# An LSTM step on one core: ScalarE writes tanh(c) into the PSUM bank of c instead of SBUF

## The chip, the cores and the metric

The kernel runs on one core of a Trainium2 chip. The metric is the device time of one execution in microseconds (us), lower is better. The engines of the core are named as in the profile: PE is the matrix engine TensorE (PEld its weight loads), DVE is VectorE, ACT is ScalarE, POOL is GpSimd, SP is the queue that issues most DMAs.

## The reference

An LSTM over a sequence of 1024 steps for a batch of two, with 256 hidden units, and behind it a mixture of experts; both are added to their inputs.

```
def step(carry, xw_t):
    prev_h, prev_c = carry
    a = xw_t + prev_h @ Wh              # 2 x 1024: gates i, f, o, g
    i, f, o = sigmoid of the first three quarters of a
    g = tanh(a[:, 3 * Hdim:])
    next_c = f * prev_c + i * g
    next_h = o * jnp.tanh(next_c)
    return ((next_h, next_c), next_h)
x = x + LSTM(x, h0=cond)                # the scan of step over 1024 steps
x = x + MoE(x, cond)                    # 2 shared and 8 routed experts, top 2
```

All arithmetic is float32. What matters here is the last line of the step: the next h is o times the tanh of the new c, and the next step can't begin its matmuls before it has h.

## The kernel before, in words

The 256 hidden units lie in two halves of 128 partitions (index m, 0 or 1). Of every half the four gates of one step stand in one PSUM tile, ps0 and ps1, 32 columns to a step's row block; 16 steps share one pair of tiles (u counts them, 0 to 15).

One step t goes through the engines like this:

- PE (L504): 20 matmuls in the order BLOCKS (L42) multiply h by Wh and add to the projected input. Each is two passes in the trace, hence 40 records of a step. The first two blocks need only the first half of h (k = 0); the third, (1, 0, 0, 128), is the first that needs the second half of h. The third ends what ps0 needs, the fifth what ps1 needs.
- DVE (L529): two transposes, ps0 and then ps1, each into the other half of the same PSUM bank.
- ACT (L532, L533): for each half the sigmoid of i, f, o and the tanh of g, read from PSUM and written into the SBUF tile `results`.
- DVE, for each half: `forget` (L536) multiplies f by the old c, which it reads from PSUM; a copy (L540, tile `seen`) waits for the tanh of g; a scan (L541) writes the new c into a PSUM tile of its half, `c0` or `c1`.
- ACT (L549, `squash_cell`): tanh of the new c, read from PSUM, written into the SBUF tile `results`. This is the line that the change touches.
- DVE (L552, `output`): o times that tanh, written into the SBUF tile h, from which PE loads the weights of the next step.

DVE has the order first forget, copy, scan; second forget, copy, scan; first output, second output. ACT has the two tanh of c behind the four activations of the gates. Both engines work strictly in the order of the code, and the waits between engines are semaphores that are counted up when an instruction is done.

c has two slots in its tile, for even and odd steps, so that the old and the new c stand side by side. The two tiles `c0` and `c1` lie in two PSUM banks of their own; the gates take four banks and the experts' work two, which makes all eight.

The experts run in the gaps. A small planner, `Fill`, keeps three queues; at each step it emits some expert matmuls for PE behind the step's own (and otherwise matmuls of zeros, L518, up to ROOM = 2 a step), some activations behind the tanh of c on ACT, and some vector work behind the outputs on DVE. A fixed budget for each step limits them. Once in 16 steps ACT also zeroes a part of the next `results` tile (L479), and POOL adds the input to h (L455).

Of the kernel before, what the change touches and what calls it, by code (L numbers as in the profile page):

```python
# [9 lines left out]
F32 = mybir.dt.float32  # L10
BF16 = mybir.dt.bfloat16
AF = mybir.ActivationFunctionType
# [4 lines left out]
P = 128  # L17
N = 2
T = 1024
D = 256  # L20
K = D // P
Q = 4
ROWS = P // Q
TB = ROWS // N
# [61 lines left out]
def lstm_moe_kernel(  # L86
# [16 lines left out]
    nc = tc.nc  # L103
# [58 lines left out]
    cells_ps = ctx.enter_context(tc.tile_pool(name="cells_ps", bufs=1, space=PSUM))  # L162
    stepp = ctx.enter_context(tc.tile_pool(name="step", bufs=3))
    stepsp = ctx.enter_context(tc.tile_pool(name="steps", bufs=2))
# [255 lines left out]
    for i in range(2):  # L420
        flat = const.tile([P, TB * DIAG], F32, name=f"h{i}")
# [4 lines left out]
    def h_at(t):  # L426
        return hs[t // TB % 2][:, t % TB]

    def h_cols(t):
        u = t % TB  # L430
        return h_at(t)[:, :, N * u : N * (u + 1)]
# [3 lines left out]
    def project(ps, grp, k):  # L435
        for m in range(K):
            for q in range(Q):
                cols = slice(q * D + m * P, q * D + (m + 1) * P)
                nc.tensor.matmul(  # L439
                    ps[m][q * ROWS : (q + 1) * ROWS],  # L440
                    one_sb if k < 0 else xT_sb[:, k, grp * TB : (grp + 1) * TB, :],
                    b_sb[:, cols] if k < 0 else wx_sb[:, k, cols],
                    start=(k < 0),
                    stop=False,
                    skip_group_check=True,
                )

    def gates_tile():

        tiles = [gates_ps.tile([P, 4, P], F32, name=f"ps{m}") for m in range(K)]  # L450
        return [a[:, 0] for a in tiles], [a[:, 1] for a in tiles], tiles[0][:, 2:]

    def residual(grp, u0, u1):
        t0 = grp * TB - 1
        nc.gpsimd.tensor_add(  # L455
            x2T[:, :, t0 + u0 : t0 + u1, :],
            xT_sb[:, :, t0 + u0 : t0 + u1, :],
            diags[grp % 2][:, u0:u1].rearrange("p u (k r) -> p k u r", r=ROWS)[:, :, :, :N],
        )
# [12 lines left out]
    nc.vector.memset(zero, 0.0)  # L472

    def results():
        flat = stepsp.tile([P, TB, K, 9 * N], F32, name="results")
        sgm = flat[:, :, :, : 6 * N].rearrange("p u m (a n z) -> p u m a n z", n=N, z=2)
        gf = flat[:, :, :, 6 * N : 8 * N].rearrange("p u m (n z) -> p u m n z", z=2)
        for m in range(K):
            nc.scalar.activation(sgm[:, :, m, 0, :, 0], zero[:, :, m], AF.Copy)  # L479
        return sgm, gf, flat[:, :, :, 8 * N :]  # L480

    nxt_results = results()

    cells = [cells_ps.tile([P, 2, N, 2], F32, name=f"c{m}") for m in range(K)]
    c_prev = [cells[m][:, 1] for m in range(K)]
    for m in range(K):
        nc.vector.memset(cells[m], 0.0)
# [5 lines left out]
    for t in range(T):  # L493
        fill.step = t
        grp, u = divmod(t, TB)
        if u == 0:
            ps, turned = nxt, nxt_turned
            nxt, nxt_turned, busy = gates_tile()
            sgm, gf, tnh = nxt_results


        for k, m, c0, c1 in BLOCKS:
            for q in range(Q):
                nc.tensor.matmul(  # L504
                    ps[m][q * ROWS : (q + 1) * ROWS][:, c0:c1],
                    h_at(t)[:, k, :],
                    wh_sb[:, k, q * D + m * P + c0 : q * D + m * P + c1],
                    start=False,
                    stop=(u == TB - 1 and k == K - 1),
                    skip_group_check=True,  # L510
                )
        ahead = t + TB < T and u in (1, 6, 11)
        if ahead:
            project(nxt, grp + 1, u // 5 - 1)
        left = max(1, due - t)
        done = fill.run_pe(-(-len(fill.pe) // left))
        for _ in range(ROOM - done - ahead):
            nc.tensor.matmul(  # L518
                busy.rearrange("p a j -> p (a j)"), busy_x[:, :P], busy_x,
                start=(u == 0), stop=False, skip_group_check=True,  # L520
            )
        rows = slice(N * u, N * (u + 1))

        gT = [turned[m].rearrange("p (a r) -> p a r", r=ROWS) for m in range(K)]
        c_new = [cells[m][:, t % 2] for m in range(K)]
        seen = [stepp.tile([P, N], F32, name=f"seen{m}") for m in range(K)]

        def transpose(m):
            nc.vector.transpose(turned[m], ps[m])  # L529

        def squash(m):
            nc.scalar.activation(sgm[:, u, m, :, :, 1], gT[m][:, 0:3, rows], AF.Sigmoid)  # L532
            nc.scalar.activation(gf[:, u, m, :, 0], gT[m][:, 3, rows], AF.Tanh)  # L533

        def forget(m):
            nc.vector.tensor_mul(gf[:, u, m, :, 1], sgm[:, u, m, 1, :, 1], c_prev[m][:, :, 1])  # L536

        def cell(m):

            nc.vector.tensor_copy(seen[m], gf[:, u, m, :, 0])  # L540
            nc.vector.tensor_tensor_scan(  # L541
                c_new[m].rearrange("p n z -> p (n z)"),
                sgm[:, u, m, 0].rearrange("p n z -> p (n z)"),
                gf[:, u, m].rearrange("p n z -> p (n z)"),
                0.0, ALU.mult, ALU.add,
            )

        def squash_cell(m):
            nc.scalar.activation(tnh[:, u, m], c_new[m][:, :, 1], AF.Tanh)  # L549

        def output(m):
            nc.vector.tensor_mul(h_cols(t + 1)[:, m], sgm[:, u, m, 2, :, 1], tnh[:, u, m])  # L552

        for fn in (transpose, squash):
            for m in range(K):
                fn(m)
        for m in range(K):
            forget(m)
            cell(m)
            squash_cell(m)  # L560
        for m in range(K):
            output(m)
        if u == TB // 2 and t + TB < T:
            nxt_results = results()
        else:
            fill.run(fill.act, 1.0)
        c_prev = c_new
        if u == TB - 1:
            residual(grp, int(grp == 0 or t - TB in ends), TB)
        if t in ends:  # L570
            residual(grp + 1, 0, 1)
            if t == T - 1:
                drain(fill)
            t0, S = ends[t]
            experts(t0, S)
            due = t + S
        if u == TB // 2 and t > TB:

            met = stepp.tile([P, 1], F32, name="met")
            nc.vector.tensor_copy(met, x2T[:, 0, t - u - 2, :1])  # L580
        fill.run(fill.dve, 0.5)
# [3 lines left out]
def drain(fill):  # L585

    while fill.pe or fill.act or fill.dve:
        fill.step += 1
        fill.run_pe(4)
        fill.run(fill.act, 100.0)  # L590
        fill.run(fill.dve, 100.0)
# [65 lines left out]
```

## Time and profile before

| | us |
|---|---|
| median of three runs | 2358.14 (2358.02 to 2358.67) |
| the execution that was profiled | 2357.18 |
| its span, first to last instruction | 2355.4 |
| PE busy | 2260.8 |
| DVE busy | 1717.5 |
| ACT busy | 917.2 |

The span has four parts: some 19 us until the first step's h, the 1024 steps up to 2299 us, and then some 56 us in which the experts of the last 64 positions are worked off. The granted clock of TensorE was 0.998 over the whole.

How to read it: PE counts as busy for nearly the whole span, but a large part of that are the matmuls of zeros and the overlapped ends of pipelined matmuls. The step is a loop through three engines, so the shares of busy time say little here; what counts is how long it takes from one h to the next. A timeline lists instructions by their start and duration, in us; in an answer on one line of code, the three durations are the least, the median and the largest in ns.

### The profile page before, as it was taken

The page shows a single profiled execution, that of the slowest core. Times are in us where ns is not written, and L with a number is a line of the kernel's source. Part 1 is how long each engine was busy: PE and PEld are TensorE (multiplying, and loading weights), DVE is VectorE, ACT ScalarE, POOL GpSimd, SP SyncE. Part 2 cuts the span into 40 slices and gives each one's busy share as a digit, 9 for nine tenths or more (in the row PEclk, how much of TensorE's full clock was granted, in tenths as well). Part 3 has the DMA queues.
Part 4 walks back from the last instruction along what each step waited for, and adds up shares of the span by engine and source line. Part 5 has one row for each costly group of instructions (what it writes and reads, how often), then busy time and mean ns, then how long its engine had stood idle before and what let it go on. Part 6 is the DMA issues. An engine that isn't in the chain of part 4 may idle for free.

```text
span 2355.4 us, 114090 instructions
## 1 busy us (share of the span) xinstructions
PE 2260.8 (96%) x48164; PEld 1604.7 (68%) x48164; DVE 1717.5 (73%) x10962; ACT 917.2 (39%) x6427; POOL 25.8 (1%) x82
## 2 busy tenths in 40 slices
PE   7999999999999999999999999999999999999998
PEld 5666666666666666666666666666666666667777
DVE  5666677777777777777777777777777777777774
ACT  3333334433444334443334433443334433344341
POOL 0000000000000000000000000000000000000000
PEclk9999999999999999999999999999999999999999
DMA  5000000000000000000000000000000000000000
GB/s 199 3 3 3 3 3 3 3 5 6 3 3 3 5 5 3 3 3 5 6 3 3 3 5 5 3 3 3 5 5 3 3 3 5 5 3 3 8 3 5
DMA packets 9412, 20.95 MB, mean 9 GB/s; under 512 B 1473, under 2 KB 6593, under 8 KB 8642
## 3 DMA queue, kind: packets, MB, share of 16 engines
q1 hardware_dynamic: 8610, 12.61, 1.5%
q8 instruction: 376, 6.16, 1.1%
q14 instruction: 138, 1.13, 0.2%
q10 hardware_dynamic: 288, 1.05, 0.1%
HBM read 11.56 MB, written 2.10 MB: 6 GB/s over the span
## 4 chain that ended last, share of the span: by engine, by line
DVE 58%; PE 39%; issue 3%; DMA 0%; SPq 0%; ACT 0%; ACTq 0%
PE ps L504 35%; DVE ps L529 28%; DVE c L541 11%; DVE results L536 8%; DVE seen L540 7%; DVE h L552 3%; PE ps_f L292 1%; PE ps_f L372 1%; PE ps_f L354 1%; DMA xT_sb<-in_xT_dram 0%; DMA wr_sb<-in_wrT_dram 0%; PE ps_f L348 0%; PE ps L518 0%; DVE acc L382 0%; PE ps L439 0%
## 5 line engine op out<-in xcount | busy, mean ns | idle before, releaser
L504 PE MATMUL ps<-wh_sb,h 128*32 128x128 f32 (+1 forms) x40960 | 1116.1, 254 | 72.4 <-DVE h L552 2.2
L504 PEld LDWEIGHTS ps<-wh_sb,h 128*32 128x32 f32 x40960 | 840.8, 109 | 477.2 <-DVE h L552 476.0
L529 DVE STREAM_TRANSPOSE ps<-ps 128x128 f32<-128x128 f32 x2048 | 676.7, 331 | 414.3 <-PE ps L504 413.1
L532 ACT ACTIVATE results<-ps 128x6 f32<-128x6 f32 x2048 | 362.5, 177 | 1178.7 <-DVE ps L529 1085.8
L518 PE MATMUL ps<-busy_x 128*128 128x256 f32 x2080 | 613.5, 392 | 0.0
L552 DVE TENSOR_TENSOR h<-results 128x2 f32<-128x2 f32 x2048 | 327.3, 160 | 175.0 <-ACT results L549 174.9
L518 PEld LDWEIGHTS ps<-busy_x 128*128 128x128 f32 x2080 | 375.4, 190 | 87.0 <-issue 46.6
L549 ACT ACTIVATE results<-c 128x2 f32<-128x2 f32 x2048 | 352.6, 172 | 205.2 <-DVE c L541 165.4
L541 DVE TENSOR_TENSOR_SCAN c<-results 128x4 f32<-128x4 f32 x2048 | 359.8, 176 | 0.0
L533 ACT ACTIVATE results<-ps 128x2 f32<-128x2 f32 x2048 | 343.5, 168 | 0.0
L540 DVE COPY seen<-results 128x2 f32<-128x2 f32 x2048 | 332.4, 162 | 0.0
L536 DVE TENSOR_TENSOR results<-results,c 128x2 f32<-128x2 f32 x2048 | 322.5, 157 | 0.0
L292 PE MATMUL ps_f<-x2T,w_sb 128*128 128x256 f32 (+1 forms) x576 | 177.0, 406 | 4.2 <-DVE h_s L315 3.4
L292 PE MATMUL ps_f<-x2T,r_sb 128*128 128x256 f32 (+1 forms) x576 | 172.5, 398 | 1.2 <-DVE h_r L335 1.0
L372 PE MATMUL ps_f<-r_sb,h_r 128*128 128x256 f32 x512 | 165.9, 421 | 0.0
L292 PEld LDWEIGHTS ps_f<-x2T,w_sb 128*128 128x128 f32 x576 | 84.8, 195 | 51.0 <-issue 46.2
L292 PEld LDWEIGHTS ps_f<-x2T,r_sb 128*128 128x128 f32 x576 | 82.5, 189 | 46.9 <-issue 45.1
L372 PEld LDWEIGHTS ps_f<-r_sb,h_r 128*128 128x128 f32 x512 | 80.4, 188 | 43.4 <-issue 39.6
L439 PE MATMUL ps<-wx_sb,xT_sb 128*32 128x128 f32 x2048 | 80.1, 275 | 3.0 <-DMA xT_sb<-in_xT_dram 3.0
L354 PE MATMUL ps_f<-w_sb,h_s 128*128 128x256 f32 x256 | 82.7, 420 | 0.0
L382 DVE SCALAR_TENSOR_TENSOR acc<-ps_f,gate,acc 128x256 f32<-128x256 f32 x128 | 61.3, 479 | 7.2 <-PE ps_f L372 6.9
L439 PEld LDWEIGHTS ps<-wx_sb,xT_sb 128*32 128x32 f32 x2048 | 59.1, 111 | 3.4 <-issue 3.4
(60 smaller groups left out, 435.1 us busy)
## 6 DMA issues: line engine op xcount, KB each, us to landing
xT_sb<-in_xT_dram SPq DMA_DIRECT2D x8, 256.0 KB, 6.5
r_sb<-in_r_w1T_dram SPq DMA_DIRECT2D x1, 2048.0 KB, 16.7
r_sb<-in_r_w2T_dram SPq DMA_DIRECT2D x1, 2048.0 KB, 18.8
out_dram<-acc SPq DMA_DIRECT2D x16, 128.0 KB, 2.1
wh_sb<-in_wh_dram ACTq DMA_DIRECT2D x2, 512.0 KB, 4.0
wx_sb<-in_wx_dram SPq DMA_DIRECT2D x2, 512.0 KB, 5.3
w_sb<-in_s_w1T_dram SPq DMA_DIRECT2D x1, 1024.0 KB, 7.2
w_sb<-in_s_w3T_dram SPq DMA_DIRECT2D x1, 1024.0 KB
```

What stands on the lines that cost most here:

```text
L292: nc.tensor.matmul(ps[:, half, :W], w[:, k, c * P : (c + 1) * P], mov[k], start=(k == 0), stop=(k == K - 1), skip_group_check=True,)
L372: nc.tensor.matmul(ps[:, half, :], toks(st["h_r"][:, c, :], i), r2_sb[:, c, :], start=(h == 0), stop=(h == HR // P - 1), skip_group_check= ...
L504: nc.tensor.matmul(ps[m][q * ROWS : (q + 1) * ROWS][:, c0:c1], h_at(t)[:, k, :], wh_sb[:, k, q * D + m * P + c0 : q * D + m * P + c1], sta ...
L518: nc.tensor.matmul(busy.rearrange("p a j -> p (a j)"), busy_x[:, :P], busy_x, start=(u == 0), stop=False, skip_group_check=True,)
L529: nc.vector.transpose(turned[m], ps[m])
L532: nc.scalar.activation(sgm[:, u, m, :, :, 1], gT[m][:, 0:3, rows], AF.Sigmoid)
L533: nc.scalar.activation(gf[:, u, m, :, 0], gT[m][:, 3, rows], AF.Tanh)
L536: nc.vector.tensor_mul(gf[:, u, m, :, 1], sgm[:, u, m, 1, :, 1], c_prev[m][:, :, 1])
L540: nc.vector.tensor_copy(seen[m], gf[:, u, m, :, 0])
L541: nc.vector.tensor_tensor_scan(c_new[m].rearrange("p n z -> p (n z)"), sgm[:, u, m, 0].rearrange("p n z -> p (n z)"), gf[:, u, m].rearrang ...
L549: nc.scalar.activation(tnh[:, u, m], c_new[m][:, :, 1], AF.Tanh)
L552: nc.vector.tensor_mul(h_cols(t + 1)[:, m], sgm[:, u, m, 2, :, 1], tnh[:, u, m])
```

## The change

The tanh of c no longer goes to the SBUF tile `results` but to a third slot of the PSUM tile of c of the same half, and the output multiply reads it there. The row of `results` shrinks from 18 to 16 floats for each step and half. A second, separate edit concerns the matmuls of zeros: of the two that stand in the first step of a group, only the first now has the flag that starts a fresh sum in the bank, and none has it behind a projection that has already set it.

```diff
     def results():
-        flat = stepsp.tile([P, TB, K, 9 * N], F32, name="results")
+        flat = stepsp.tile([P, TB, K, 8 * N], F32, name="results")
-        gf = flat[:, :, :, 6 * N : 8 * N].rearrange("p u m (n z) -> p u m n z", z=2)
+        gf = flat[:, :, :, 6 * N :].rearrange("p u m (n z) -> p u m n z", z=2)
...
-        return sgm, gf, flat[:, :, :, 8 * N :]
+        return sgm, gf
...
-    cells = [cells_ps.tile([P, 2, N, 2], F32, name=f"c{m}") for m in range(K)]
+    cells = [cells_ps.tile([P, 3, N, 2], F32, name=f"c{m}") for m in range(K)]
...
-            sgm, gf, tnh = nxt_results
+            fresh = True
+            sgm, gf = nxt_results
...
             project(nxt, grp + 1, u // 5 - 1)
+            fresh = False
...
-                start=(u == 0), stop=False, skip_group_check=True,
-            )
+                start=fresh, stop=False, skip_group_check=True,
+            )
+            fresh = False
...
         def squash_cell(m):
-            nc.scalar.activation(tnh[:, u, m], c_new[m][:, :, 1], AF.Tanh)
+            nc.scalar.activation(cells[m][:, 2, :, 0], c_new[m][:, :, 1], AF.Tanh)
 
         def output(m):
-            nc.vector.tensor_mul(h_cols(t + 1)[:, m], sgm[:, u, m, 2, :, 1], tnh[:, u, m])
+            nc.vector.tensor_mul(h_cols(t + 1)[:, m], sgm[:, u, m, 2, :, 1], cells[m][:, 2, :, 0])
```

## The prediction, made before the run

> **What bounds the kernel now.** I read the chain of waits first, then the groups by line, then the timeline of one ordinary step, then the start and duration of every record of the lines of the step (all ns below are medians or means over those 1,024 steps).
>
> ```profile
> DVE 58%; PE 39%; issue 3%; DMA 0%; SPq 0%; ACT 0%; ACTq 0%
> ...
> L552 DVE TENSOR_TENSOR h<-results 128x2 f32<-128x2 f32 x2048 | 327.3, 160 | 175.0 <-ACT results L549 174.9
> ...
> L549 ACT ACTIVATE results<-c 128x2 f32<-128x2 f32 x2048 | 352.6, 172 | 205.2 <-DVE c L541 165.4
> ```
>
> The chain is the loop from h to h, 2,220 ns in the median step, and the page gives ACT no share of it. That is the first thing to test, since the change makes nothing but ACT's tanh of c (L549) and its reader (L552) different. One step, DVE and then ACT:
>
> ```profile
> 1001.23 0.66 DVE L529 STREAM_TRANSPOSE ps<-ps 128x128 f32<-128x128 f32 x2 [0.55 <-PE ps L504]
> ...
> 1002.14 0.16 DVE L536 TENSOR_TENSOR results<-results,c 128x2 f32<-128x2 f32 x1
> 1002.21 0.16 DVE L540 COPY seen<-results 128x2 f32<-128x2 f32 x1
> 1002.33 0.17 DVE L541 TENSOR_TENSOR_SCAN c<-results 128x4 f32<-128x4 f32 x1
> 1002.41 0.16 DVE L552 TENSOR_TENSOR h<-results 128x2 f32<-128x2 f32 x1
> 1002.74 0.16 DVE L552 TENSOR_TENSOR h<-results 128x2 f32<-128x2 f32 x1 [0.17 <-ACT results L549]
> ```
>
> ```profile
> 1002.21 0.17 ACT L549 ACTIVATE results<-c 128x2 f32<-128x2 f32 x1
> 1002.53 0.17 ACT L549 ACTIVATE results<-c 128x2 f32<-128x2 f32 x1 [0.16 <-DVE c L541]
> ```
>
> The second output (1002.74) starts 32 ns behind the end of the second tanh: it waits for ACT, plainly. The first output (1002.41) starts 83 ns behind the start of the second scan in every ordinary step (82 to 85), so the page puts it down to DVE. But in the same records it also starts only 32 to 39 ns behind the end of the first tanh. Which of the two holds it? Its end tells: by how early the first tanh was, the steps sort into
>
> - gap of 33 ns to the tanh's end: duration 160, end 243 behind the scan's start (113 steps)
> - gap of 35: duration 159, end 242 (336 steps)
> - gap of 37: duration 156, end 239.5 (50 steps)
> - gap of 38: duration 156, end 239 (36 steps)
>
> The end stays 193 to 194 ns behind the tanh's end, whatever the start. So **the first output is held by ACT too**, by its end though not by its start, and a shorter tanh would bring h earlier. How far, steps show in which the tanh had long been done: 22 times the second scan took 254 to 258 ns in place of 175, and the output behind it then had a duration of 143 to 145 and ended 59 ns behind the scan's end; in steps 0 and 1 it ended 58 and 62 behind. Ordinary steps have 66.8. So DVE itself would let go of h **7.8 ns** earlier, and no more.
>
> From h, PE's loads follow at once: 53 ns behind the end of the first output in nearly all steps. The third block needs the second half of h, and here is a second, small stall: where the second output ends up to 277 ns behind that first load, the step's last matmul starts at +815; above that it slips ns for ns (280: +818). The mean is 279.4, the mean slip **2.4 ns** a step.
>
> **The change part by part.** By the two kernels' lists of instructions no instruction is added, removed or moved on any engine, and each keeps the semaphore it waits for. There are 2,048 tanh with another destination and 2,048 multiplies with another source.
>
> *The multiply.* `forget` (L536) already has the form that L552 gets: one operand in SBUF, the other in PSUM, 128x2, output to SBUF, held by ACT.
>
> ```profile
> L536 DVE TENSOR_TENSOR results<-results,c x2048: 143/157/160, 18.5 to 2298.9; 128x2 f32<-128x2 f32 x187
> ...
> L552 DVE TENSOR_TENSOR h<-results x2048: 143/160/164, 19.1 to 2299.5; 128x2 f32<-128x2 f32 x187
> ```
>
> From the end of the activation to its own end `forget` takes 190 ns, L552 193.5. I take -3.5 ns for each multiply. [...] The rows of this trace differ: 157 with PSUM against 160 without.
>
> *The tanh.* No row has ACT writing PSUM, so its price is bounded from both sides. What ACT saves when its source is PSUM: the sigmoid L236 reads SBUF and takes 208 ns for 16 elements; L309 to L330 (378 ns at 256 elements, 592 at 512) give 0.84 ns an element, so 195 remain; L549 from PSUM has 172 - 2 = 170. That is 25 ns; were the destination worth as much, the tanh would take 147. On the other side DVE: its scan, which writes PSUM, ends 92 ns behind the next start (175 - 83), its multiply, which writes SBUF, 83 (160 - 77, to the work behind the second output), so a write to PSUM costs DVE 9 or 10 ns more. I take a gain of 15 ns, nearer to the row of the same engine; the bounds are +25 and -10. [...]
>
> *The sum for one step.* The first tanh ends 48 ns behind the second scan's start, the output 193.5 later: 242. After: 48 - 15 + 190 = 223, but DVE allows no less than 242 - 7.8 = 234. The gain is 7.8; any tanh shorter by 4 ns gives it all. The second output ends 15 + 3.5 earlier, the first load 7.8 earlier, so the second is 10.7 earlier against it, 268.7 in place of 279.4: under 277, and the 2.4 ns of PE's stall go too (from 7 ns of gain on). Together 10.2 ns. What is late next is the second scan, through the second transpose: it stands on PE's last matmul and on the first transpose, which come 10.2 earlier with everything else, and on no part of ACT that changes.
>
> Steps that have it: all but the 22 with the long scan, which have only the 2.4, and about 20 of the last 64, which take 2.5 to 2.9 us because expert matmuls fill PE. That leaves some 980 steps: 980 x 10.2 = **10.0 us**. The drain of 56 us behind the last step is not touched.
>
> *At nothing:* the memset of c grows from 8 to 12 columns (65 ns now, twice, while the first loads are under way); uncovered it is some 8 ns once. The flag of the zero matmuls changes no duration that a row distinguishes. The rows of `results` are 64 bytes apart in place of 72; medians by place in the group differ by 1 or 2 ns in L532 and L536, which is 2 us either way and stands in the range.
>
> On the profiled execution 2357.18 - 10.0 = 2347.2; it lies 1.0 under the median of the runs, so the median should go from 2358.14 to **2348**.
>
> **The rivals.**
>
> 1. *The destination is worth nothing to ACT, or the page is right that ACT is off the chain.* With 0 from the tanh only the 3.5 of the multiply stay, 3.4 us: 2354.7. If the second scan alone held the first output, the 2.4 of PE alone would go: 2355.8. Against the second reading stands the row of gaps and ends; nothing excludes the first.
> 2. *ACT's write to PSUM is answered later* (slower than before). The price is DVE's 10 ns. Both outputs then come 10 - 3.5 = 6.5 later, and nothing hides it, since DVE's own floor is passed: 6.4 us, 2364.5; without the 3.5, 2368. It decides as soon as the tanh is over 4 ns longer than now. For it: ACT would read and write the same bank, which no row shows.
> 3. *VectorE is late on a PSUM operand that another engine has just written.* The transposes start 68 ns behind the modelled end of PE's last matmul, 35 more than the 33 that DVE has behind ACT. Then 48 - 15 + 193.5 + 35 = 262, 20 over now: 2378. Against it: ACT starts 33 ns behind DVE's writes to PSUM. [...]
> 4. *DVE's floor is lower.* The shortest multiplies take 143; at a start of +83 that ends at 226, not 234: 16 + 2.4 ns, 18 us, 2340. It needs a gain of 12 or more from the tanh.
>
> **How the numbers follow.** Forecast 0.55, with its own range 2344 to 2351 (the floor of 58 to 62 ns, the 2 us of the rows of `results`); rival 1 0.17, rival 2 0.15, rival 3 0.06, rival 4 0.07. Faster by over 0.2% (4.7 us, about what a measurement of this kernel can tell from no change) are the forecast and rival 4, 0.62; within it rival 1, 0.17; slower rivals 2 and 3, 0.21. The range is 2340 to 2365: it leaves out rival 3 and the upper part of rival 2.
>
> **What would show it.** In the profile after: the tanh at some 157 ns (147 to 182 are the bounds); the output's durations under 160, the first one's near 150, and its start still 83 behind the second scan; the end of the first output 234 behind that start; the second output under 277 ns behind the first load; the median step near 2,210 ns. A tanh of 172 makes it rival 1, of 180 rival 2; a gap from tanh to second output well over 32 ns rival 3. I am wrong if the first output's end is not ACT's to move, or if the tanh is no shorter.

## The result and the profile after

The changed kernel takes **2345.62 us** in the median of six runs (2344.69 to 2346.22), the kernel before 2358.13 in six runs beside it: a ratio of 0.9946, 95% interval 0.9933 to 0.9959. That is 12.5 us less; 10.0 were forecast. The profiled execution took 2345.25 us, span 2343.5, against 2357.18 and 2355.4: 11.9 less.

The page after, chain of waits and groups by line (the tanh of c is now L552, the output L555, the transposes L532, PE's step matmuls L505):

```profile
DVE 58%; PE 38%; issue 3%; DMA 1%; ACT 0%; SPq 0%; ACTq 0%
...
L555 DVE TENSOR_TENSOR h<-results,c 128x2 f32<-128x2 f32 x2048 | 313.8, 153 | 168.4 <-ACT c L552 168.3
...
L552 ACT ACTIVATE c<-c 128x2 f32<-128x2 f32 x2048 | 321.5, 157 | 220.0 <-DVE c L544 180.1
```

The chain gives ACT 0% before and after, although nothing but ACT's instruction and its reader got faster: the mean tanh went from 172 ns to 157, the mean output from 160 to 153. One step in the timeline, DVE and then ACT:

```profile
1001.40 0.17 DVE L544 TENSOR_TENSOR_SCAN c<-results 128x4 f32<-128x4 f32 x1
1001.48 0.15 DVE L555 TENSOR_TENSOR h<-results,c 128x2 f32<-128x2 f32 x1
1001.80 0.16 DVE L555 TENSOR_TENSOR h<-results,c 128x2 f32<-128x2 f32 x1 [0.17 <-ACT c L552]
```

```profile
1001.28 0.16 ACT L552 ACTIVATE c<-c 128x2 f32<-128x2 f32 x1
1001.61 0.16 ACT L552 ACTIVATE c<-c 128x2 f32<-128x2 f32 x1 [0.17 <-DVE c L544]
```

The first output still starts 0.08 us behind the second scan and the page still names no releaser for it; only its duration is shorter, 0.15 in place of 0.16. The gain stands in the ends of the records, as the answers by line show (least, median and largest duration in ns behind the count):

```profile
L552 ACT ACTIVATE c<-c x2048: 157/157/157, 19.6 to 2287.8; 128x2 f32<-128x2 f32 x187
...
L555 DVE TENSOR_TENSOR h<-results,c x2048: 144/156/157, 19.8 to 2287.9; 128x2 f32<-128x2 f32 x187
```

From the records of the ordinary steps (no change of group, no expert backlog), means in ns. "Stall" is how much later than +815 the step's last matmul starts behind its first load:

| kernel | tanh, first/second half | first output's end behind the second scan's end | the same behind its own tanh's end | second output's end behind its tanh's end | second output's end behind PE's first load | stall | step |
|---|---|---|---|---|---|---|---|
| before | 172/172 | 66.9 | 193.5 | 193.6 | 279.2 | 2.4 | 2219.4 |
| after | 157/157 | 58.5 | 199.1 | 188.5 | 267.8 | 0.0 | 2208.3 |
| tanh_alone | 157/157 | 58.6 | 198.7 | 187.9 | 267.0 | 0.0 | 2209.5 |
| first_half_same_layout | 157/172 | 58.4 | 198.8 | 193.4 | 287.3 | 11.0 | 2217.9 |
| second_half_same_layout | 172/157 | 65.4 | 193.0 | 188.5 | 260.5 | 0.0 | 2216.9 |
| first_late_8 | 161/157 | 58.5 | 196.1 | 188.4 | 267.7 | 0.0 | 2208.3 |
| first_late_28 | 174/157 | 70.8 | 189.0 | 188.4 | 255.2 | 0.0 | 2220.8 |
| second_late | 157/164 | 58.5 | 196.8 | 188.6 | 299.4 | 22.6 | 2229.3 |
| multiply_alone | 172/172 | 62.3 | 188.3 | 188.5 | 278.9 | 3.0 | 2216.2 |

The experiments below fill this table. Its use: against before, the change in column three plus the change in the stall should be the change of the step. After: -8.4 - 2.4 = -10.8, measured -11.1. In the other rows the sum and the measured difference lie at most 1.9 apart.

### The profile page after: what moved, and what is told of

Same layout as the page of the kernel before. It is cut to its first block, busy times and chain, and to the rows that moved or that the text cites. A ratio compares the mean times of both kernels' runs of the same rounds, so it can differ in the third digit from the quotient of the medians.

```text
span 2343.5 us, 114090 instructions
## 1 busy us (share of the span) xinstructions
PE 2256.0 (96%) x48164; PEld 1600.0 (68%) x48164; DVE 1704.1 (73%) x10962; ACT 886.9 (38%) x6427; POOL 25.8 (1%) x82
## 4 chain that ended last, share of the span: by engine, by line
DVE 58%; PE 38%; issue 3%; DMA 1%; ACT 0%; SPq 0%; ACTq 0%
PE ps L505 35%; DVE ps L532 28%; DVE c L544 11%; DVE results L539 8%; DVE seen L543 7%; DVE h L555 3%; PE ps_f L292 1%; PE ps_f L372 1%; PE ps_f L354 1%; DMA xT_sb<-in_xT_dram 0%; DMA wr_sb<-in_wrT_dram 0%; DVE h_r L335 0%; PE ps_f L348 0%; DVE acc L382 0%; ACT er L330 0%
## 5 line engine op out<-in xcount | busy, mean ns | idle before, releaser
L505 PE MATMUL ps<-wh_sb,h 128*32 128x128 f32 (+1 forms) x40960 | 1112.8, 254 | 64.0 <-DVE h L555 1.0
L505 PEld LDWEIGHTS ps<-wh_sb,h 128*32 128x32 f32 x40960 | 837.7, 109 | 468.6 <-DVE h L555 467.5
L532 DVE STREAM_TRANSPOSE ps<-ps 128x128 f32<-128x128 f32 x2048 | 678.0, 332 | 421.9 <-PE ps L505 420.6
L555 DVE TENSOR_TENSOR h<-results,c 128x2 f32<-128x2 f32 x2048 | 313.8, 153 | 168.4 <-ACT c L552 168.3
L552 ACT ACTIVATE c<-c 128x2 f32<-128x2 f32 x2048 | 321.5, 157 | 220.0 <-DVE c L544 180.1
```

Source lines behind the costliest of these rows:

```text
L505: nc.tensor.matmul(ps[m][q * ROWS : (q + 1) * ROWS][:, c0:c1], h_at(t)[:, k, :], wh_sb[:, k, q * D + m * P + c0 : q * D + m * P + c1], sta ...
L552: nc.scalar.activation(cells[m][:, 2, :, 0], c_new[m][:, :, 1], AF.Tanh)
```

## The experiments

**Theory.** The step is a loop from h to h. The end of the first output is held by the later of two things: its own tanh's end and VectorE's own floor, some 58 ns behind the second scan's end. The second output holds PE only when it ends over 277 ns behind the first load. The shorter tanh moves both outputs, and only both together give the gain. **Rivals:** the other edits (rows of 64 bytes, flags of the zero matmuls) carry a part; the halves simply add up; the page is right that ACT is off the chain; VectorE pays for an operand in PSUM.

**The tanh alone.** On the kernel before, only this:

```diff
-    cells = [cells_ps.tile([P, 2, N, 2], F32, name=f"c{m}") for m in range(K)]
+    cells = [cells_ps.tile([P, 3, N, 2], F32, name=f"c{m}") for m in range(K)]
...
-            nc.scalar.activation(tnh[:, u, m], c_new[m][:, :, 1], AF.Tanh)
+            nc.scalar.activation(cells[m][:, 2, :, 0], c_new[m][:, :, 1], AF.Tanh)
...
-            nc.vector.tensor_mul(h_cols(t + 1)[:, m], sgm[:, u, m, 2, :, 1], tnh[:, u, m])
+            nc.vector.tensor_mul(h_cols(t + 1)[:, m], sgm[:, u, m, 2, :, 1], cells[m][:, 2, :, 0])
```

> Only the destination of the tanh and the source of the multiply are changed; rows of results stay 72 bytes apart and the flags of the zero matmuls stay. Theory (a 15 ns shorter tanh through two holds: DVE's floor behind the second scan, and PE's stall): all of the gain, 12.5 us under before, 2345 to 2347. Rival (part of the gain is the 64-byte rows or the flags): 1 to 4 us of it missing, 2347 to 2350.

Measured: 2345.88 us (before 2357.82 beside it), ratio 0.995 [0.9937, 0.9962]. That is 11.9 less, nearly all of the gain; the step of 2209.5 ns leaves about 1 ns for everything else. The tanh there:

```profile
L549 ACT ACTIVATE c<-c x2048: 157/157/157, 19.3 to 2288.7; 128x2 f32<-128x2 f32 x187
```

**The rest alone, and one half alone.** On the changed kernel the tanh of c goes into an SBUF tile of its own, for both halves (rest_alone), for the second (first_half) or for the first (second_half):

```diff
+        tnh = stepsp.tile([P, TB, K, N], F32, name="tnh")
...
-            nc.scalar.activation(cells[m][:, 2, :, 0], c_new[m][:, :, 1], AF.Tanh)
+            nc.scalar.activation(tnh[:, u, m], c_new[m][:, :, 1], AF.Tanh)
```

> Everything else is changed, but the tanh stays in SBUF, in a tile of its own. Theory: no change beyond 2 us, 2356 to 2360, tanh 172 ns, output 160. Rival (rows or flags carry part): 1 to 4 us under before.

> Only the first half's tanh goes to PSUM. Theory: the first output ends 8 ns earlier, but the second does not, so it ends 287 to 288 ns behind the first load and the last matmul slips by 10 in place of 2.4; the step gains nothing or at most 1 ns, 2356 to 2358. Rival (halves add up, each half brings half): 2352. Rival (the first output alone sets the step): 2347 to 2350.

> Only the second half's tanh goes to PSUM. Theory: the first output is unchanged, 67 ns behind the scan's end; PE's stall of 2.4 ns goes; 2.4 us under before, 2355.5. Rival (halves add up): 2352. With the first half alone near 0 and this near 2.4, the two together must exceed their sum by some 9 us.

Measured: 2360.0 (1.0009 [1.0, 1.0017]), 2358.43 (1.0003 [0.9994, 1.0012]) and 2358.39 (1.0003 [0.9994, 1.0012]) against 2357.82. All three are longer than they should be, for a reason that the edit itself brought. The answer for the tanh's line in rest_alone:

```profile
L553 ACT ACTIVATE tnh<-c x2048: 172/172/174, 19.6 to 2302.2; 128x2 f32<-128x2 f32 x187
L553 ACTq EVENT_SEMAPHORE  x55: 17/17/17, 91.7 to 2268.5; - x55
```

ACTq is the profile's name for ACT's own sequencer. The first use of a fresh `tnh` tile has a second semaphore to wait for, 55 times here and in each of the other two runs, and then the tanh starts 94 ns behind its scan's end, not 34: 55 x 60 ns = 3.3 us. Without it rest_alone would be some 1 us under before. Measured from rest_alone, which carries the same tile, each half alone is worth 1.6 us. Since the tile itself costs more than that, I ran the halves again on the old layout, with no new tile.

**One half alone, on the layout of before.** As tanh_alone, but only for m = 0 (or m = 1); the other half keeps SBUF:

```diff
+            nc.scalar.activation(cells[m][:, 2, :, 0] if m == 0 else tnh[:, u, m], c_new[m][:, :, 1], AF.Tanh)
...
+            nc.vector.tensor_mul(h_cols(t + 1)[:, m], sgm[:, u, m, 2, :, 1], cells[m][:, 2, :, 0] if m == 0 else tnh[:, u, m])
```

> The kernel before with its layout of results kept, and only the first half's tanh to PSUM; no second wait on any tanh, which cost 60 ns in 55 steps of the run with a tile of its own. Theory: first output 8 ns earlier, second output late by the same against it (287 to 288 ns behind the first load), PE's slip 10 in place of 2.4: 2357 to 2358. Rival (halves add up): 2352.

> The same with the second half alone. Theory: no slip at PE, first output unchanged: 2.4 ns a step, 2355 to 2356. Rival (halves add up): 2352.

Measured: first half 2356.31 us (0.9998 [0.9989, 1.0006]), second half 2352.74 (0.9982 [0.9973, 0.9991]), before 2356.99. The gains are 0.7 and 4.2, in sum 4.9, where both together give 11.9 to 12.5: **not additive**. The 4.2 are more than the 2.4 expected, and the time by itself lies at the rival's 2352. The step does not: it is 2.5 ns shorter, as the theory has it, and the profiled execution took 2354.35, 2.8 under that of before. What the median has beyond that stays open. The first_half_same_layout answers show both kinds side by side:

```profile
L549 ACT ACTIVATE c<-c x1024: 157/157/157, 19.5 to 2298.1; 128x2 f32<-128x2 f32 x171
L549 ACT ACTIVATE results<-c x1024: 172/172/174, 19.8 to 2298.4; 128x2 f32<-128x2 f32 x171
```

```profile
L552 DVE TENSOR_TENSOR h<-results,c x1024: 143/148/156, 19.7 to 2298.3; 128x2 f32<-128x2 f32 x171
L552 DVE TENSOR_TENSOR h<-results x1024: 160/161/164, 20.0 to 2298.7; 128x2 f32<-128x2 f32 x171
```

With the first half alone the first output does come 8.5 ns earlier (66.9 to 58.4), but the second output does not, PE's first load is earlier against it, and the stall grows from 2.4 to 11.0: +8.6 takes -8.5 back. With the second half alone only the stall goes.

**Delaying one tanh in the changed kernel.** A copy on ACT ahead of one half's tanh, n columns of a constant into an unused tile, makes that tanh late: n = 56 and 80 at m = 0, 231 at m = 1.

```diff
+            if m == 0:
+                nc.scalar.activation(junk[:, :80], busy_x[:, :80], AF.Copy)
             nc.scalar.activation(cells[m][:, 2, :, 0], c_new[m][:, :, 1], AF.Tanh)
```

> The changed kernel with a copy of 56 zeros on ACT in front of the first tanh, meant to make it start some 8 ns later. Theory (DVE's floor holds the first output, which leaves the first tanh 10 ns): no change against the changed kernel, 2345 to 2347. Rival (the output follows the tanh without a floor): 8 us more, 2354.

> The same with 80 zeros, some 28 ns later. Theory: the first 10 ns are free, the other 18 come through: 2362 to 2364, and the output ends 188 to 189 ns behind the tanh again in place of 199. Rival without a floor: 28 us more, 2373. Rival (ACT is off the chain, as the page has it): 2346.

Measured: 2345.1 us (0.9948 [0.9935, 0.996]) and 2356.59 (0.9998 [0.9989, 1.0007]); before 2356.99. Both delays came out smaller than I set them, so the second time missed the 2362 to 2364 expected, and each is read by its measured delay. Against the second scan's end, the tanh of first_late_8 ended only 3 ns later than in the changed kernel, and nothing changed: it was inside the free room, which is 199.1 - 188.5 = 10.6 ns. In first_late_28 it ended 22.4 ns later: its record starts some 6 ns later and has 174 ns in place of 157. The theory then gives 22.4 - 10.6 = 11.8; the step is 12.5 longer, where it would be 22 without the floor. The whole gain is gone. Its page and its answer for the output:

```profile
DVE 58%; PE 38%; issue 3%; DMA 0%; ACT 0%; SPq 0%; ACTq 0%
```

```profile
L558 DVE TENSOR_TENSOR h<-results,c x2048: 143/156/158, 19.1 to 2300.8; 128x2 f32<-128x2 f32 x187
```

The chain still gives ACT 0% and DVE 58%, in a kernel that is 11 us longer by ACT alone. The first output ends 189.0 ns behind its tanh, the distance that the second output has to its tanh wherever it reads PSUM: ACT holds it. That refutes the rival that believes the page.

> The changed kernel with a copy of 231 zeros on ACT in front of the second tanh; by the two runs with a late first tanh it should end some 22 ns later. Theory (PE's third block holds the second half: 277 ns behind the first load, and it stands at 268, so 9 are free): 13 ns a step, 2357 to 2359, PE's slip 12 to 14. Rival without that room: 22 a step, 2367. Rival (only the first output counts): 2346.

Measured: 2366.0 us (1.0038 [1.0024, 1.0052]), before 2357.14: 20.4 over the changed kernel, more than expected. The delay had come out larger than I set it: the tanh started 25 ns late and took 164 ns in place of 157, so the second output ended 299.4 ns behind the first load, 31.6 later. By the theory 277 - 267.8 = 9.2 of that are free and 22.4 are PE's; the stall measured 22.6, the step 21.0. So the threshold held, and my setting of the delay missed. The time alone would have misled: it lies at the 2367 of the rival without that room. But by the measured delay that rival asks for a step 31.6 longer.

**The multiply alone.** On the kernel before, the tanh stays in SBUF and the output multiplies it by c in PSUM in place of the sigmoid of o in SBUF, so this kernel leaves out the output gate:

```diff
-            nc.vector.tensor_mul(h_cols(t + 1)[:, m], sgm[:, u, m, 2, :, 1], tnh[:, u, m])
+            nc.vector.tensor_mul(h_cols(t + 1)[:, m], tnh[:, u, m], c_new[m][:, :, 1])
```

> The kernel before, tanh to SBUF, but the multiply takes the new c in PSUM in place of the sigmoid of o in SBUF: h is c times tanh(c), which leaves out the output gate. Theory: a PSUM operand beside an SBUF one costs the multiply nothing and ends it 3.5 to 5 ns sooner behind the tanh: 3 to 5 us under before, the tanh still 172. Rival (VectorE pays for PSUM): slower than before. If the 5 ns belong to the tanh's write alone: as before.

Measured: 2353.58 us (0.9982 [0.9973, 0.9991]), before 2357.14: 3.6 less. In the answers the tanh is the old one and the output is shorter:

```profile
L549 ACT ACTIVATE results<-c x2048: 172/172/173, 19.7 to 2296.3; 128x2 f32<-128x2 f32 x187
```

```profile
L552 DVE TENSOR_TENSOR h<-results,c x2048: 142/156/159, 19.9 to 2296.5; 128x2 f32<-128x2 f32 x187
```

Its end comes 188.4 ns behind the tanh's in place of 193.5. An operand in PSUM costs this multiply nothing; it gains 5 ns.

**The sigmoid too.** If a destination in PSUM is worth 15 ns to ACT wherever the loop waits for ACT, then the sigmoid is the next place. On the changed kernel, the sigmoid of i and f goes into the bank of c; that of o follows the tanh of g as an activation of its own into SBUF; c is copied to SBUF behind the outputs, so that `forget` multiplies i and f by an SBUF operand at once. The zeroing of `results` (L479) is no longer needed and left out:

```diff
-            nc.scalar.activation(sgm[:, u, m, :, :, 1], gT[m][:, 0:3, rows], AF.Sigmoid)
+            nc.scalar.activation(sgm[m][:, :, :, 1], gT[m][:, 0:2, rows], AF.Sigmoid)
             nc.scalar.activation(gf[:, u, m, :, 0], gT[m][:, 3, rows], AF.Tanh)
+            nc.scalar.activation(og[:, u, m], gT[m][:, 2, rows], AF.Sigmoid)
...
+        for m in range(K):
+            nc.vector.tensor_copy(c_sb[m], c_new[m][:, :, 1])
```

> The changed kernel, and the sigmoids of i and f go to the PSUM bank of c as well; the sigmoid of o is an activation of its own into SBUF, forget reads a copy of c in SBUF that DVE makes behind the outputs (and multiplies i by c too, which nobody uses), and the zeroing of results on ACT falls away. Theory: the sigmoid of the second half stands on DVE's chain without any floor behind it, so its 15 ns come through in full, 14 to 16 us under the changed kernel, 2330 to 2332; less (2334 to 2338) where forget of the first half is held by the second transpose. Rival (the two more copies on DVE or the third activation on ACT collide with the step): no faster than the changed kernel.

Measured: **2330.27 us** (2329.17 to 2330.69), ratio to before 0.9886 [0.9872, 0.9899], 15.3 under the changed kernel: it beats both. Groups by line, the sigmoid of i and f and `forget`:

```profile
L532 ACT ACTIVATE c<-ps 128x4 f32<-128x4 f32 x2048 | 323.6, 158 | 1139.2 <-DVE ps L529 1109.5
...
L537 DVE TENSOR_TENSOR results<-c,c_sb 128x4 f32<-128x4 f32 x2048 | 320.2, 156 | 0.0
```

The sigmoid has 158 ns where it had 177 (with 4 columns in place of 6), `forget` takes no longer for twice the elements (156 ns), and in the ordinary steps the second scan ends 1257.6 ns behind the first transpose's start in place of 1271.7: 14.1 of a step that is 14.5 shorter. Some 1.7 us of the 15.3 come from elsewhere: the 21 steps in which the second scan takes 257 ns in place of 175 are not there in this run (see the last section). Several things changed at once here, so the run shows that the next step pays, not what the sigmoid's destination alone is worth.

**Another bank.** On the changed kernel, each half's tanh goes into the bank that holds c of the other half:

```diff
-            nc.scalar.activation(cells[m][:, 2, :, 0], c_new[m][:, :, 1], AF.Tanh)
+            nc.scalar.activation(cells[1 - m][:, 2, :, 0], c_new[m][:, :, 1], AF.Tanh)
...
-            nc.vector.tensor_mul(h_cols(t + 1)[:, m], sgm[:, u, m, 2, :, 1], cells[m][:, 2, :, 0])
+            nc.vector.tensor_mul(h_cols(t + 1)[:, m], sgm[:, u, m, 2, :, 1], cells[1 - m][:, 2, :, 0])
```

> The changed kernel with the tanh of each half written into the bank that holds c of the other half, and the output multiply reading it there. While the first tanh runs, VectorE's forget, copy and scan of the second half read and write that other bank. If the destination PSUM alone makes the tanh 15 ns shorter, and neither the source's bank nor a neighbour on the bank matters: tanh 157 ns for both halves, first output 58 to 59 ns behind the second scan's end, median step 2208 to 2209, time 2344 to 2347. If the saving comes from reading and writing one bank: tanh 172, median step near 2217 (the multiply's 5 ns stay), time 2352 to 2355. If two engines on one bank at the same time hold each other up: the second scan above 175 ns or the first tanh above 157, and the step longer by as much as the scan, for each 10 ns some 10 us over the changed kernel.

Measured: 3052.36 us, ratio 1.2963 [1.2945, 1.2981]. None of the three times was near. The answers by line for `forget`, the tanh and the output, with the idle time ahead of them (us, times) and its releaser:

```profile
L539 DVE TENSOR_TENSOR results<-results,c x2048: 143/156/159, 18.8 to 2995.8; 128x2 f32<-128x2 f32 x187
its engine sat idle before it (us, times) until:
  ACT c L552: 290.8, 1024
```

```profile
L552 ACT ACTIVATE c<-c x2048: 157/157/157, 19.2 to 2996.3; 128x2 f32<-128x2 f32 x187
L552 ACTq EVENT_SEMAPHORE  x2047: 17/17/17, 19.8 to 2996.2; - x187
its engine sat idle before it (us, times) until:
  DVE c L544: 506.9, 1030
```

```profile
L555 DVE TENSOR_TENSOR h<-results,c x2048: 148/154/158, 20.1 to 2996.5; 128x2 f32<-128x2 f32 x187
...
  ACT c L552: 292.2, 1024
```

The tanh has 157 ns here too, against 172 with SBUF, so the saving belongs to a PSUM destination and not to the bank of its source. Whether a neighbour on the bank stretches an instruction, the third question, stays open: the two engines now take turns on it. The 696 ns a step are waits. The two tanh now touch both banks, and so `forget` of the second half, which reads c of that half, stands behind the first tanh, which writes other columns of the same bank: it starts 318 ns later. Every tanh but one has a second semaphore to wait for and starts 94 ns behind its scan's end, not 34. The first output stands behind the second tanh and ends 439 ns behind the second scan in place of 58.5. 380 there and 315 up to that scan's end make the 696 ns by which the step is longer, but for 1. My expectation had overlooked that the program as built has waits between instructions on different columns of one bank: the first output and the second tanh both only read the bank of c1, in different columns, and still one waits for the other (L555 on L552, 1,024 times, 292.2 us). Each of the two banks holds one tile, so whether the order goes by bank or by tile can't be told from this run, and what would happen without these waits no run here shows. In the bank of the same half all these orders are there already: scan, tanh and output of a half follow each other anyway.

## Why the prediction was right, and where its sizes were off

- **The tanh, 15 ns.** Measured 172 to 157, all 2,048: the value taken between the bounds of +25 and -10. That it came out to the nanosecond is luck, and the sum did not need it: by its own terms any gain over 7 gives the same. The row of the same engine, ACT's saving with a source in PSUM, was the better pointer; DVE's 10 ns had the wrong sign.
- **The multiply, -3.5 ns.** Mis-sized: -5.1 in multiply_alone, both halves. In the changed kernel that changes nothing for the first output, which stands on DVE's floor; the second ends 188.5 ns behind its tanh in place of 193.6.
- **The first output of the kernel before is held by ACT, though the page of the profile calls it DVE's.** Shown by first_late_28 from one side and by tanh_alone from the other.
- **The floor, 7.8 ns.** Measured 8.4. It is the term that bounds the gain. Against the second scan's end the first tanh ends 14.0 earlier, the multiply gives 5.0 more; of these 19.0 ns the floor lets 8.4 through, and the rest is the free room of 10.6.
- **PE's stall, 2.4 ns.** Gone, as forecast: second output 267.8 behind the first load (268.7 forecast). The threshold of 277 came out in second_late once more, at 22.4 against 22.6.
- **The step.** 2208.3 (about 2,210 forecast), 11.1 ns less where 10.2 were summed. 0.6 of the difference is the floor; the remaining 0.3 could be the rows of 64 bytes, by which `forget` of the second half went from 158.0 to 156.8, but that was not measured by itself.
- **The number of steps.** I took 980 steps; all steps from the third on are together 11.1 us shorter. The start with the first two steps gives 0.5 more, the drain 0.3: the 11.9 of the two profiled executions. No run shows that these 0.8 come from the change: over all the runs the second step takes between 2.2 and 3.5 us and the drain between 53.2 and 55.7. The 12.5 of the medians has 0.6 more, since the profiled execution of before lay 1.0 under its median and that of after 0.4. (The long scans that the prediction counts as 22 are 21.)

Of the rivals, 1 (nothing from the tanh) and 2 (ACT's write later) fall with the 157; 3 (VectorE late on PSUM written by another engine) with the gap to the second output, still 32 ns; 4 (a floor 16 ns lower, some 51) with the 58.5.

## What to carry to other kernels

In a loop of short instructions over several engines, read the *ends* of the records against each candidate's end before you believe the chain: an instruction that starts on time can still be held by another engine, as the first output here: in both kernels it starts 83 ns behind the second scan's start, but in the kernel before its end stood 193.5 ns behind its tanh's, as that of the second output did (193.6), which plainly waits for ACT. Then ask of every link how much it can give before the next one holds, and whether two links must move together, as the two halves here (0.7 and 4.2 us alone, 11.9 to 12.5 together). When a result is moved into PSUM, look first at which engines touch that bank between its write and its read: the right bank was worth 12.5 us here, the wrong one cost 697.

## What the runs showed of the hardware that I had not expected

- A second semaphore wait on the tanh cost far more here than its own record of 17 ns: the tanh started 60 ns later (94 ns behind its scan's end in place of 34), in 55 steps of rest_alone and in nearly all of other_bank.
- The same tanh into PSUM, 157 ns in every step of the changed kernel, has a record of 174 ns in first_late_28, of 161 in first_late_8 and of 164 in second_late, with a copy just ahead of it on ACT. Why is not shown. So durations of one form can't be compared here without what went ahead, and a delay has to be measured at the end of the delayed record.
- In 21 steps of before and after the second scan takes 254 to 258 ns in place of 175. In each of them POOL's addition (L455) runs across it, and the scan ends 28 to 33 ns behind POOL's end. In gates_too the second scan runs across the same addition 21 times and keeps 174 ns; there one of its two sources lies in PSUM. So it looks as if this scan, with both sources in SBUF, is held until POOL is done, which no run tests by itself. The first two lines are from after, the others from gates_too:

```profile
371.24 0.35 POOL L455 TENSOR_TENSOR x2T<-xT_sb,h 128x64 f32<-128x64 f32 x1 [36.40 <-DVE c L544]
371.36 0.26 DVE L544 TENSOR_TENSOR_SCAN c<-results 128x4 f32<-128x4 f32 x1
```

```profile
369.93 0.35 POOL L455 TENSOR_TENSOR x2T<-xT_sb,h 128x64 f32<-128x64 f32 x1 [36.14 <-DVE c L545]
370.04 0.17 DVE L545 TENSOR_TENSOR_SCAN c<-c,results 128x4 f32<-128x4 f32 x1
```
